# The end of an attention kernel rewritten: the last seven steps of the software pipeline in another order, a third buffer and other PSUM banks for the outputs

## The chip, the cores and the metric

The kernel runs on one core of one Trainium2 chip. The metric is the device time of one execution in microseconds (us). Before the change the median of three runs is 1626.83 us. An engine of the core (TensorE or PE, VectorE or DVE, ScalarE or ACT, GpSimd or POOL, SyncE or SP) works off its own instructions in the order in which they were emitted, and waits at an instruction until what that instruction needs is there.

## The reference

```python
x = L0_attn_x                                       # (2, 2048, 256), float32
x = x + rnn(layernorm(x), Wi, bi, Wh, bh)            # h = tanh(xt + h @ Wh.T + bh), along 2048 steps
x = x + ffn(layernorm(x), Wq, Wk, Ws, Wd, Wv, Wo)

# ffn: 8 heads of 64, 5 experts of which 2 are chosen
q, k = heads of x @ Wq, x @ Wk
wv = topk_mask(x @ Ws, 2) * sigmoid(x @ Ws)          # per token, head, expert
v = einsum('bthe,btek->bhtk', wv, einsum('btd,edk->btek', x, Wv))
probs = softmax(q * 64**-0.5 @ k.T)
attn = probs @ v
out = einsum('bthe,bthk,ekd->btd', topk_mask(x @ Wd, 2), attn, Wo)
```

## The kernel before

The first 130 us or so compute the recurrent part. Everything after it is attention, and it is one long software pipeline written out by hand: the order of the instructions in the program is the order in which each engine works.

**Units and steps.** There are 2 batches x 8 heads = 16 heads, and each head has 4 blocks of 512 queries: 64 units `u`. A unit works through the 2048 keys in 8 tiles `t` of 256 keys each (two halves of 128, side by side in a 128 x 1024 tile). A step `T` takes two such tiles, so a unit has `U_T` = 4 steps and there are `NT` = 256 steps with new scores, T = 0 to 255. A tile's way is:

- step T: `scores` (PE, line 634, into the PSUM pool `ps_s` of two buffers, tag "s"), `stage` (ACT copies the scores to SBUF, line 645), `largest` (DVE keeps a running maximum);
- after the unit's last tile: `turn_max`, `reduce_max`, `spread_max` turn the maxima into a 128 x 512 tile `top`. For the last unit the PSUM tile `pt` of it takes a buffer of "s", because no scores follow;
- step T+5: `subtract` takes the maximum off (line 693). POOL does most of them. DVE does the first two of each unit, and in the last unit every even one, reading `pt`;
- `exponential` (ACT, line 696): of the first tile of a pair at the end of step T+5, of the second at the start of step T+6;
- step T+6 (`LAG` = 6): `products` (PE, line 706: v times the probabilities, into `o`), and `fold` (POOL issues a DMA that adds one tile of a pair into the other, line 718), after which `sums` (PE, line 727) counts the denominators into `d` at every second step. The last unit has no folds; its sums go straight from the tiles.

So after the last scores at T = 255 there are seven more steps, T = 256 to 262, that only work off what is under way. In them the tiles 500 to 511 go through `products`; tiles 504 to 511 belong to the last unit, 63.

**Closing a unit.** `take` copies `o` to SBUF (lines 742, 743), `take_sums` the denominators (ACT line 749, DVE line 750). `close` calls `weigh`, which transposes the result (PE, line 759, tile `po` in a bank of the PSUM pool `misc`, two buffers) and forms the weights (DVE, lines 761 to 768), and multiplies them into `pro`, one copy for each expert (DVE, line 772). `gather` adds `pro` into `yd` in DRAM by a DMA, or, for the last head, adds it (POOL, line 817) to the tile `y` that `fetch_y` brought back (SP, line 793, 640 KB). For unit 63 `close_last` does it in four slices, each a product and an addition on DVE (lines 772 and 804).

**Outputs.** With the last head of a batch closed, each of its 16 chunks `c` of 128 tokens goes through `turn_out` and `project_out`. `turn_out(b, c)` makes three PE transposes of `y` into `py` (line 829, a `misc` bank), two ACT copies to SBUF (lines 833, 836), and issues on SP the load of the residual `z` (line 838, 128 KB). `project_out(b, c)` makes 24 matmuls into `pz` (line 846, a `misc` bank), the addition `z` = `pz` + `z` (DVE, line 854) and the store of `z` (SP, line 855, 128 KB). The tile `z` has two buffers: a load waits on SP until the store of the chunk two before it has landed, and SP's later transfers wait behind it.

**Order.** The lists `before`, `first_behind` and `behind` hold, for each step T, what is done before its products and behind its sums. For the last four units (chunks 0 to 15 of the second batch) the order before the change is:

| step T | before its products | behind its sums |
| --- | --- | --- |
| 256 | project 1 | `spread_max(63)`, close unit 61 |
| 257 | turn 2 | project 2, turn 3, gather unit 61 |
| 258 | project 3 | turn 4, fetch y of unit 62 |
| 259 | project 4 | take sums of unit 62, turn 5 |
| 260 | project 5 | close unit 62 |
| 261 | turn 6 | project 6, turn 7, gather unit 62, fetch y of unit 63 |
| 262 | project 7 | turn 8, turn 9, project 8, take sums and close unit 63, then turn and project the rest in turns, to chunk 15 |

`choose`, early in each batch, makes the experts' ranks: DVE writes the comparisons `later1` to `later4` (line 236), POOL counts them (lines 241, 242).

Of the kernel before, what the change touches and what calls it, by code (L numbers as in the profile page):

```python
# [8 lines left out]
F32 = mybir.dt.float32  # L9
# [5 lines left out]
P = 128  # L15
# [5 lines left out]
def rnn_then_switchhead_kernel(  # L21
# [15 lines left out]
    nc = tc.nc  # L37
    B, T, D = x.shape
    E, _, DH = Wv.shape
    H = Wq.shape[1] // DH  # L40
    KC = D // P
    NCH = T // P
    NP = H // 2
    QB = 512
    NQ = T // QB
    QS = QB // P
# [13 lines left out]
    for c in range(NCH):  # L60
        t = rconst.tile([P, B, D], F32, tag=f"x{c}", name=f"x{c}")
# [39 lines left out]
    o_chunks = [(i, min(P, ED - i)) for i in range(0, ED, P)]  # L101
# [18 lines left out]
    def misc(shape, nm):  # L120
        return ps_m.tile(shape, F32, tag="m", name=nm)
# [95 lines left out]
    def choose(pool, b, c0, n, half, nm, logits):  # L217

        gl = gates_all[:, c0 : c0 + n, b, half * HE : (half + 1) * HE]
        g = gl.rearrange("p c (h e) -> p c h e", e=E)
        nc.scalar.copy(logits, gl)
        g0 = logits.rearrange("p c (h e) -> p c h e", e=E)
        rank = pool.tile([P, n, H, E], F32, tag="rank", bufs=1, name=f"rank{nm}")
        nc.gpsimd.tensor_copy(
            rank.rearrange("p c h e -> p (c h) e"),
            ramp.unsqueeze(1).to_broadcast([P, n * H, E]),
        )
        if not half:  # L230
            sg = pool.tile([P, n, HE], F32, tag="sg", bufs=2, name=f"sg{nm}")
            nc.scalar.activation(sg, gl, AF.Tanh, scale=0.5)
        later = []
        for d in range(1, E):
            a = pool.tile([P, n, H, E - d], F32, tag=f"later{d}", bufs=1 + (d > 1), name=f"lt{nm}_{d}")
            nc.vector.tensor_tensor(a, g0[:, :, :, d:E], g[:, :, :, 0 : E - d], ALU.is_gt)
            later.append(a)

        def count(d):
            lo, hi = rank[:, :, :, 0 : E - d], rank[:, :, :, d:E]  # L240
            nc.gpsimd.tensor_tensor(lo, lo, later[d - 1], ALU.add)
            nc.gpsimd.tensor_tensor(hi, hi, later[d - 1], ALU.subtract)

        def take():
            rank_ = rank.rearrange("p c h e -> p c (h e)")
            if half:
                nc.gpsimd.tensor_scalar(gl, rank_, 1.5, None, ALU.is_lt)
                return

            nc.gpsimd.tensor_scalar(sg, sg, 0.5, 0.5, ALU.mult, ALU.add)  # L250
            nc.gpsimd.tensor_scalar(rank_, rank_, 1.5, None, ALU.is_lt)
            nc.gpsimd.tensor_tensor(gl, rank_, sg, ALU.mult)

        return [lambda d=d: count(d) for d in range(1, E)] + [take]
# [15 lines left out]
    with tc.tile_pool(name="prep", bufs=3) as pp, tc.tile_pool(  # L270
        name="lna", bufs=3
    ) as lnp, tc.tile_pool(name="ps_xi", bufs=3, space=PSUM) as ps_xi, tc.tile_pool(
        name="ps_t", bufs=3, space=PSUM
# [284 lines left out]
    LAG = U_T + 2  # L558
# [7 lines left out]
    NT = len(units) * U_T  # L566
# [121 lines left out]
    def subtract(t):  # L688
        u, c = t // HC, t % HC
        p = ring[t]  # L690
        last = u == len(units) - 1 and c % 2 == 0
        eng, top = (nc.vector, top_of[u][0]) if c < 2 or last else (nc.gpsimd, top_of[u][1])
        eng.tensor_tensor(p, p, top.unsqueeze(1).to_broadcast([P, 2, QB]), ALU.subtract)  # L693

    def exponential(t):
        nc.scalar.activation(ring[t], ring[t], AF.Exp)  # L696
# [95 lines left out]
        y_of[b, n] = four.tile([P, QS, E, DH], F32, tag="y", bufs=2, name=f"y{b}_{n}")  # L792
        nc.sync.dma_start(out=y_of[b, n], in_=yd[b, n])

    def close_last(u):

        i, n = units[u]
        b, _ = heads[i]
        po, mr = weigh(u)
        y = y_of[b, n]  # L800
        pr = four.tile([P, QS, E, DH], F32, tag="pro", bufs=1, name=f"pro{u}")
        for s in range(QS):
            masked(pr[:, s : s + 1], po, mr, s, 1)
            nc.vector.tensor_tensor(y[:, s], y[:, s], pr[:, s], ALU.add)

    def gather(u):

# [14 lines left out]
    for yT in yT_all:  # L822
        nc.gpsimd.memset(yT[:, len(o_chunks) - 1, :], 0.0)

    def turn_out(b, c):
        yf = y_of[b, c // QS][:, c % QS].rearrange("p e k -> p (e k)")
        py = misc([P, len(o_chunks), P], f"py{b}_{c}")
        for k, (r0, m) in enumerate(o_chunks):
            nc.tensor.transpose(py[0:m, k, :], yf[:, r0 : r0 + m], ident)
        yT = yT_all[yT_of["n"] % 2]  # L830
        yT_of["n"] += 1
        full = sum(m == P for _, m in o_chunks)
        nc.scalar.copy(yT[:, 0:full, :], py[:, 0:full, :])
        for k, (r0, m) in enumerate(o_chunks):
            if m < P:
                nc.scalar.copy(yT[0:m, k, :], py[0:m, k, :])
        z = ap.tile([P, D], F32, tag="z", name=f"z{b}_{c}")
        nc.sync.dma_start(out=z, in_=x1d[c, :, b, :])
        yT_of[b, c] = (yT, z)

# [75 lines left out]

    def at(table, T, f, *a):
        table.setdefault(T, []).append(lambda: f(*a))
# [58 lines left out]
    for u, (i, n) in enumerate(units):  # L977
        b, h = heads[i]
        T1 = (u + 1) * U_T
        at(first_behind, T1, spread_max, u)  # L980
        outs = [(b, n * QS + s) for s in range(QS)]
        if u == len(units) - 1:

            outs = [(b, c) for c in range(n * QS - QS, n * QS + QS)]
            todo = [(turn_out, *outs[0])]
            for k, o in enumerate(outs):
                todo += [(turn_out, *x) for x in outs[k + 1 : k + 2]] + [(project_out, *o)]
            at(behind, T1 + LAG - 1, fetch_y, u)
            for x in todo[:3] + [(take_sums, u), (close_last, u)] + todo[3:]:
                at(behind, T1 + LAG, *x)  # L990
            continue
        at(behind, T1 + LAG + 1, take_sums, u)
        at(behind, T1 + LAG + 2, close, u)
        at(behind, T1 + LAG + 3, gather, u)
        if h == H - 1:
            at(behind, T1 + LAG, fetch_y, u)
            if u < len(units) - 2:
                T = T1 + LAG + 4
                for o, t, p in zip(outs, (0, 1, 3, 3), (1, 2, 3, 4)):
                    at(before if o[1] % QS == 2 else behind, T + t, turn_out, *o)  # L1000
                    at(behind if o[1] % QS == 2 else before, T + p, project_out, *o)

    with tc.manual_schedule():
        for T in range(NT + LAG + 1):
            new = (2 * T, 2 * T + 1) if T < NT else ()
            sub = [t for t in (2 * (T - LAG + 1), 2 * (T - LAG + 1) + 1) if 0 <= t < 2 * NT]
            old = [t for t in (2 * (T - LAG), 2 * (T - LAG) + 1) if 0 <= t < 2 * NT]
            u_old = (T - LAG) // U_T - 1
            done = (T - LAG) % U_T == 0 and 0 <= u_old < len(units)
            fresh = sub and sub[0] % HC == 0  # L1010
            if done:
                take(u_old)
            if old:
                exponential(old[1])

            ss = [scores(t) for t in new]
            if new:
                stage(new[0], ss[0])
            if T % U_T == 0:
                if new:  # L1020
                    stage(new[1], ss[1])
                if 0 < T <= NT:
                    turn_max(T // U_T - 1)
                    reduce_max(T // U_T - 1)
                if new:
                    largest(new[1], ss[1])
            elif new:
                largest(new[1], ss[1])
                stage(new[1], ss[1])
            if fresh:  # L1030
                subtract(sub[0])
            if T % U_T and new:
                largest(new[0], ss[0])
            if fresh:
                subtract(sub[1])
            if sub and not fresh:
                subtract(sub[0])
            k = T - LAG
            if 0 < k < NT - U_T + 1:
                fold(2 * (k - 1))  # L1040
            if sub and not fresh:
                subtract(sub[1])
            for f in before.pop(T, []):
                f()
            for t in old:
                products(t)
            if 3 <= k and k % 2 and k - 3 < NT - U_T:
                t = 2 * (k - 3)
                sums(t, t + 2, t % HC == 0, t % HC != 0)
            if NT - 2 <= k < NT:  # L1050

                t0 = 2 * (NT - U_T)
                for t in range(t0, t0 + 4, 2) if k == NT - 2 else ():
                    sums(t, t + 1, t == t0, False)
                sums(2 * k, 2 * k + 1, False, k == NT - 1)
            if sub:
                exponential(sub[0])
            for f in first_behind.pop(T, []) + behind.pop(T, []):
                f()
        assert not before and not behind and not first_behind  # L1060
# [46 lines left out]
```

## Time and profile before

| what | value |
| --- | --- |
| three runs | 1624.53, 1626.83, 1630.81 us; median 1626.83 us |
| the profiled execution | 1623.28 us, its span in the profile 1621.5 us |
| mean granted TensorE clock | 0.992 of full speed |
| PE busy | 1539.0 us, 95% of the span |
| DVE, ACT, POOL busy | 1296.5, 1250.2, 1284.8 us (80%, 77%, 79%) |
| `z` loads | 32 of 128 KB, median 2.5 us from issue to landing |
| `z` stores | 32 of 128 KB, median 1.9 us |
| folds | 252 of 512 KB, median 6.2 us |
| `y` loads | 8 of 640 KB, median 6.8 us |

The profile is of one execution. A row of the timeline or of the groups gives the start, the duration, the engine, the line of the kernel, the operation, the tile written and the tile read, the shapes, and in square brackets how long the engine stood idle before it and who ended that. PEld is the loading of weights into PE, which overlaps its matmuls. A busy PE need not be a PE at its peak. "Landing" is the time from a DMA's issue to its completion.

### The profile page before, as it was taken

The numbers are of one execution on the slowest core, as the hardware profiler recorded it, in microseconds if no ns is written. First come the engines' busy times: TensorE is split into PE (matmuls) and PEld (weight loads), VectorE is DVE, ScalarE is ACT, GpSimd is POOL, SyncE is SP. The second block draws the span as 40 slices with busy tenths as digits, with TensorE's granted clock in tenths as the row PEclk, the third lists the DMA queues.
The fourth block names the chain that finished last, engine by engine and source line by source line (L and its number), as shares of the span: only waits on it lengthen the run. The fifth ranks groups of instructions, "written<-read, shape, count | busy, mean of one in ns | idle before, by whom it ended". The sixth has DMA issues, their size and how long they took to land.

```text
span 1621.5 us, 29233 instructions
## 1 busy us (share of the span) xinstructions
PE 1539.0 (95%) x11442; PEld 594.1 (37%) x11442; DVE 1296.5 (80%) x1807; ACT 1250.2 (77%) x1616; POOL 1284.8 (79%) x857
## 2 busy tenths in 40 slices
PE   6989899999999999998999999999999999999996
PEld 5974223333333333333333333333333333333333
DVE  7473789998988887777887768898888888988763
ACT  4664678888888888777887768888888888888862
POOL 3054688888888988888998768898889899998980
PEclk9999999999999999999999999999999999999999
DMA  5021368788888888677886767788888888889762
GB/s 161 1 106 37 106 141 193 176 188 173 178 172 172 173 168 172 139 166 143 180 182 156 174 148 178 168 169 174 169 172 169 178 160 177 168 174 186 153 134 86
DMA packets 86624, 252.27 MB, mean 156 GB/s; under 512 B 11920, under 2 KB 31184, under 8 KB 86480
## 3 DMA queue, kind: packets, MB, share of 16 engines
q0 software_dynamic: 43200, 163.60, 53.9%
q1 hardware_dynamic: 41648, 86.13, 17.6%
q8 instruction: 92, 1.51, 0.4%
q10 hardware_dynamic: 1632, 0.61, 0.1%
q14 instruction: 52, 0.43, 0.1%
HBM read 59.46 MB, written 50.33 MB: 68 GB/s over the span
## 4 chain that ended last, share of the span: by engine, by line
PE 64%; DVE 15%; DMA 6%; ACT 3%; issue 3%; POOL 1%; SPq 0%; DVEq 0%; ACTq 0%
PE s L634 23%; PE o L706 20%; DVE m L655 6%; PE d L727 6%; PE pq L159 4%; PE pk L140 3%; ACT p L645 3%; DMA xq<-xvd 2%; DMA p<-p 2%; PE pz L846 2%; DVE pro L772 2%; PE pt L683 2%; PE pm L668 1%; DVE p L693 1%; PE po L759 1%
## 5 line engine op out<-in xcount | busy, mean ns | idle before, releaser
L693 POOL TENSOR_TENSOR p<-p,top 128x1024 f32<-128x1024 f32 x381 | 1053.6, 3002 | 4.8 <-ACT top L686 4.6
L645 ACT COPY p<-s 128x1024 f32<-128x1024 f32 x512 | 511.0, 1011 | 161.4 <-DVE m L655 70.1
L696 ACT ACTIVATE p<-p 128x1024 f32<-128x1024 f32 x512 | 538.1, 1062 | 47.8 <-DVE p L693 38.1
L634 PE MATMUL s<-qs,k 64*128 64x512 f32 x1024 | 511.3, 617 | 7.7 <-ACT p L645 7.7
L634 PE MATMUL s<-q,k 64*128 64x512 f32 x1024 | 511.3, 617 | 6.7 <-ACT p L645 5.9
L706 PE MATMUL o<-p,v 128*32 128x512 f32 x4096 | 492.0, 597 | 8.5 <-DVE os L743 6.4
L655 DVE TENSOR_TENSOR m<-s,m 128x1024 f32<-128x1024 f32 x320 | 390.7, 1221 | 78.3 <-PE s L634 69.1
L718 POOL DMA_DIRECT2D p<-p x252 | 339.8, 1348 | 69.7 <-ACT p L696 22.9
L706 PEld LDWEIGHTS o<-p,v 128*32 128x32 f32 x4096 | 114.6, 109 | 297.2 <-issue 157.7
L634 PEld LDWEIGHTS s<-qs,k 64*128 64x128 f32 x1024 | 168.8, 185 | 145.3 <-issue 49.2
L634 PEld LDWEIGHTS s<-q,k 64*128 64x128 f32 x1024 | 168.8, 185 | 141.9 <-issue 49.6
L693 DVE TENSOR_TENSOR p<-p,pt 128x1024 f32<-128x1024 f32 x131 | 158.4, 1210 | 0.1
L727 PE MATMUL d<-p,ones 128*32 128x512 f32 x1040 | 151.5, 594 | 1.7 <-DMA p<-p 1.7
L655 DVE TENSOR_TENSOR m<-s,p 128x1024 f32<-128x1024 f32 x64 | 78.4, 1224 | 53.8 <-ACT p L645 53.4
L814 POOL DMA_DIRECT2D yd<-pro x48 | 43.3, 903 | 94.1 <-DVE pro L772 90.2
L619 DVE TENSOR_TENSOR xq<-xq,wp 128x1280 f32<-128x1280 f32 x60 | 89.2, 1487 | 28.3 <-DMA xq<-xvd 26.5
L772 DVE TENSOR_TENSOR pro<-po,mr 128x1280 f32<-128x1280 f32 (+1 forms) x67 | 95.9, 1431 | 2.7
L625 DVE TENSOR_REDUCE v<-xq 128x256 f32<-128x1280 f32 x60 | 88.6, 1476 | 0.0
L159 PE MATMUL pq<-xn2T,wq 128*32 128x512 f32 x512 | 66.8, 635 | 12.8 <-DVE xq L619 8.7
L727 PEld LDWEIGHTS d<-p,ones 128*32 128x32 f32 x1040 | 37.8, 110 | 91.9 <-issue 77.0
L140 PE MATMUL pk<-xn2T,wk 128*32 128x512 f32 x512 | 61.5, 598 | 0.7 <-ACT q L169 0.7
L673 DVE TENSOR_REDUCE mq<-pm 128x4 f32<-128x512 f32 x64 | 44.3, 692 | 19.2 <-PE pm L668 17.8
(175 smaller groups left out, 1472.4 us busy)
## 6 DMA issues: line engine op xcount, KB each, us to landing
p<-p POOLq DMA_DIRECT2D x252, 512.0 KB, 6.2
xq<-xvd SPq DMA_DIRECT2D x60, 640.0 KB, 5.2
yd<-pro POOLq DMA_DIRECT2D x48, 640.0 KB, 7.5
qs<-q SPq DMA_DIRECT2D x64, 128.0 KB, 2.7
yd<-pro SPq DMA_DIRECT2D x8, 640.0 KB, 4.1
y<-yd SPq DMA_DIRECT2D x8, 640.0 KB, 6.8
x<-in_x SPq DMA_DIRECT2D x16, 256.0 KB, 5.5
x1d<-x SPq DMA_DIRECT2D x16, 256.0 KB, 2.0
```

Of the source, the lines that this page charges most:

```text
L140: nc.tensor.matmul(pk[at_col : at_col + 32], lhsT=wk[:, kc, h * DH + g : h * DH + g + 32], rhs=xc[:, kc, c0 // 2 : (c0 + HC) // 2, o, :], ...
L159: nc.tensor.matmul(pq[at_col : at_col + 32, :], lhsT=wq[:, kc, h * DH + g : h * DH + g + 32], rhs=xn2T[:, kc, b, n * QB : (n + 1) * QB], s ...
L619: nc.vector.tensor_tensor(xq, xq, wp.unsqueeze(2).to_broadcast([P, 4, DH, E]), ALU.mult)
L634: nc.tensor.matmul(ss[:, o, :], lhsT=k_of[i][half, c, :], rhs=q_of[i, n][o][half, :], start=True, stop=True,)
L645: nc.scalar.copy(p, ss)
L655: nc.vector.tensor_tensor(m, ss, ring[t - 1] if c == 1 else m, ALU.max)
L693: eng.tensor_tensor(p, p, top.unsqueeze(1).to_broadcast([P, 2, QB]), ALU.subtract)
L696: nc.scalar.activation(ring[t], ring[t], AF.Exp)
L706: nc.tensor.matmul(o_of[u][at_col : at_col + 32, :], lhsT=v_of[i][:, 2 * c + o, g : g + 32], rhs=ring[t][:, o, :], start=c == 0, stop=c == ...
L718: nc.gpsimd.dma_start(out=ring[t], in_=ring.pop(t + 1), accum_op=ALU.add)
L727: nc.tensor.matmul(den_of[u][32 * g : 32 * (g + 1), :], lhsT=ones32, rhs=ring[(t, t1)[g // 2]][:, g % 2, :], start=first, stop=last, tile_ ...
L772: nc.vector.tensor_tensor(dst, po[:, s : s + n, 0:DH].unsqueeze(2).to_broadcast([P, n, E, DH]), mr[:, s : s + n].unsqueeze(3).to_broadcast ...
```

## The change

Only the order of the last seven steps and the buffers they use are changed; what is computed is the same.

- The exponentials of both tiles of a step follow their subtractions in the same step (T = 257, 258). At T = 259 the subtractions of tiles 508 to 511 are all made, and their four exponentials; T = 260 has none.
- Unit 61 is gathered at T = 256 and not 257; unit 62 is closed and gathered at T = 259, in the step of its sums, and not at 260 and 261. The `y` of unit 63 is fetched at T = 260 and not 261.
- Outputs go in pairs: chunks 4 and 5 are turned behind T = 258 and projected at 259, 6 and 7 at 259 and 260, 8 and 9 at 260 and 261, 10 and 11 at 261 and 262. Chunks 12 to 15 follow the closing of unit 63.
- The transposes `py` of chunks 4, 6, 8, 10 and 12 to 15 go to the two "s" buffers of the scores' pool; chunks 5, 7, 9 and 11 stay in `misc`.
- `z` has three buffers and not two; `later4` has one and not two.

```diff
--- before.py
+++ after.py
@@ -232,7 +232,7 @@
             nc.scalar.activation(sg, gl, AF.Tanh, scale=0.5)
         later = []
         for d in range(1, E):
-            a = pool.tile([P, n, H, E - d], F32, tag=f"later{d}", bufs=1 + (d > 1), name=f"lt{nm}_{d}")
+            a = pool.tile([P, n, H, E - d], F32, tag=f"later{d}", bufs=1 + (1 < d < 4), name=f"lt{nm}_{d}")
             nc.vector.tensor_tensor(a, g0[:, :, :, d:E], g[:, :, :, 0 : E - d], ALU.is_gt)
             later.append(a)
 
@@ -792,7 +792,7 @@
         y_of[b, n] = four.tile([P, QS, E, DH], F32, tag="y", bufs=2, name=f"y{b}_{n}")
         nc.sync.dma_start(out=y_of[b, n], in_=yd[b, n])
 
-    def close_last(u):
+    def close_last(u, outs):
 
         i, n = units[u]
         b, _ = heads[i]
@@ -802,6 +802,11 @@
         for s in range(QS):
             masked(pr[:, s : s + 1], po, mr, s, 1)
             nc.vector.tensor_tensor(y[:, s], y[:, s], pr[:, s], ALU.add)
+        for s in range(QS):
+            turn_out(*outs[s], True)
+            if s:
+                project_out(*outs[s - 1])
+        project_out(*outs[-1])
 
     def gather(u):
 
@@ -822,9 +827,14 @@
     for yT in yT_all:
         nc.gpsimd.memset(yT[:, len(o_chunks) - 1, :], 0.0)
 
-    def turn_out(b, c):
+    def turn_out(b, c, spare=False):
         yf = y_of[b, c // QS][:, c % QS].rearrange("p e k -> p (e k)")
-        py = misc([P, len(o_chunks), P], f"py{b}_{c}")
+        if spare:
+
+            py = ps_s.tile([P, 2, QB], F32, tag="s", name=f"py{b}_{c}")[:, 0, : len(o_chunks) * P]
+            py = py.rearrange("p (k n) -> p k n", n=P)
+        else:
+            py = misc([P, len(o_chunks), P], f"py{b}_{c}")
         for k, (r0, m) in enumerate(o_chunks):
             nc.tensor.transpose(py[0:m, k, :], yf[:, r0 : r0 + m], ident)
         yT = yT_all[yT_of["n"] % 2]
@@ -834,7 +844,7 @@
         for k, (r0, m) in enumerate(o_chunks):
             if m < P:
                 nc.scalar.copy(yT[0:m, k, :], py[0:m, k, :])
-        z = ap.tile([P, D], F32, tag="z", name=f"z{b}_{c}")
+        z = ap.tile([P, D], F32, tag="z", bufs=3, name=f"z{b}_{c}")
         nc.sync.dma_start(out=z, in_=x1d[c, :, b, :])
         yT_of[b, c] = (yT, z)
 
@@ -980,25 +990,34 @@
         at(first_behind, T1, spread_max, u)
         outs = [(b, n * QS + s) for s in range(QS)]
         if u == len(units) - 1:
-
-            outs = [(b, c) for c in range(n * QS - QS, n * QS + QS)]
-            todo = [(turn_out, *outs[0])]
-            for k, o in enumerate(outs):
-                todo += [(turn_out, *x) for x in outs[k + 1 : k + 2]] + [(project_out, *o)]
-            at(behind, T1 + LAG - 1, fetch_y, u)
-            for x in todo[:3] + [(take_sums, u), (close_last, u)] + todo[3:]:
-                at(behind, T1 + LAG, *x)
+            at(behind, T1 + LAG - 2, fetch_y, u)
+            at(behind, T1 + LAG, take_sums, u)
             continue
         at(behind, T1 + LAG + 1, take_sums, u)
+        if h == H - 1:
+            at(behind, T1 + LAG, fetch_y, u)
+        if u == len(units) - 2:
+            at(behind, T1 + LAG + 1, close, u)
+            at(behind, T1 + LAG + 1, gather, u)
+            continue
         at(behind, T1 + LAG + 2, close, u)
+        if u == len(units) - 3:
+            at(behind, T1 + LAG + 2, gather, u)
+            continue
         at(behind, T1 + LAG + 3, gather, u)
         if h == H - 1:
-            at(behind, T1 + LAG, fetch_y, u)
-            if u < len(units) - 2:
-                T = T1 + LAG + 4
-                for o, t, p in zip(outs, (0, 1, 3, 3), (1, 2, 3, 4)):
-                    at(before if o[1] % QS == 2 else behind, T + t, turn_out, *o)
-                    at(behind if o[1] % QS == 2 else before, T + p, project_out, *o)
+            T = T1 + LAG + 4
+            for o, t, p in zip(outs, (0, 1, 3, 3), (1, 2, 3, 4)):
+                at(before if o[1] % QS == 2 else behind, T + t, turn_out, *o)
+                at(behind if o[1] % QS == 2 else before, T + p, project_out, *o)
+
+    last = [(B - 1, c) for c in range(NCH - 3 * QS, NCH)]
+    for k in range(0, 2 * QS, 2):
+        T = NT + 2 + k // 2
+        for o in last[k : k + 2]:
+            at(behind, T, turn_out, *o, o[1] % 2 == 0)
+            at(behind if T == NT + LAG - 1 else before, T + 1, project_out, *o)
+    at(behind, NT + LAG, close_last, len(units) - 1, last[2 * QS :])
 
     with tc.manual_schedule():
         for T in range(NT + LAG + 1):
@@ -1010,7 +1029,7 @@
             fresh = sub and sub[0] % HC == 0
             if done:
                 take(u_old)
-            if old:
+            if old and T < NT + 2:
                 exponential(old[1])
 
             ss = [scores(t) for t in new]
@@ -1033,13 +1052,17 @@
                 largest(new[0], ss[0])
             if fresh:
                 subtract(sub[1])
-            if sub and not fresh:
+            if sub and not fresh and T < NT + LAG - 2:
                 subtract(sub[0])
             k = T - LAG
             if 0 < k < NT - U_T + 1:
                 fold(2 * (k - 1))
-            if sub and not fresh:
+            if sub and not fresh and T < NT + LAG - 2:
                 subtract(sub[1])
+            if T == NT + LAG - 3:
+
+                subtract(sub[0] + 2)
+                subtract(sub[1] + 2)
             for f in before.pop(T, []):
                 f()
             for t in old:
@@ -1053,8 +1076,13 @@
                 for t in range(t0, t0 + 4, 2) if k == NT - 2 else ():
                     sums(t, t + 1, t == t0, False)
                 sums(2 * k, 2 * k + 1, False, k == NT - 1)
-            if sub:
+            if sub and T < NT + LAG - 2:
                 exponential(sub[0])
+            if NT < T < NT + LAG - 2:
+                exponential(sub[1])
+            if T == NT + LAG - 3:
+                exponential(sub[0] + 2)
+                exponential(sub[1] + 2)
             for f in first_behind.pop(T, []) + behind.pop(T, []):
                 f()
         assert not before and not behind and not first_behind
```

## The prediction

> **What bounds the kernel now.** I read the page, the stretches around the end, the waits of the last stretch, the chain of waits, and the timeline of the last 65 us. The page first:
>
> ```profile
> span 1621.5 us, 29233 instructions
> PE 1539.0 (95%) x11442; PEld 594.1 (37%) x11442; DVE 1296.5 (80%) x1807; ACT 1250.2 (77%) x1616; POOL 1284.8 (79%) x857
> ```
>
> PE fills the span, so an edit of the end is worth what PE stands idle there. T = 256 begins near 1556.5 us; the last sums (T = 261) end at 1588.33 (issued 1587.29, 1.04 long). The two stretches:
>
> ```profile
> 1556.50:1588.33 31.83, 29.16 (x306) 11.96 (x306) 14.65 (x22) 16.48 (x27) 18.68 (x11) 1.00 0.55 130
> 1588.33:1621.50 33.17, 20.72 (x272) 10.23 (x263) 9.73 (x23) 5.86 (x20) 2.23 (x1) 0.90 0.29 96
> ```
>
> The columns are the length, then PE, PEld, DVE, ACT and POOL busy, clock, DMA share, GB/s. In the first stretch PE idles 2.7 us, in the second 12.5. What it waits for there, from the waits of the second stretch and the chain:
>
> ```profile
> DVE z L854 <- DMA z<-x1d: 13.1, 6, 3.1
> SPq L838 <- DMA out<-z: 11.3, 7, 1.9
> ```
>
> ```profile
> 1611.15 2.13 DMA out<-z
> ...
> 1613.35 0.32 SPq L838
> ...
> 1613.71 2.24 DMA out<-z
> ...
> 1615.96 2.05 DMA z<-x1d
> ...
> 1618.14 0.42 DVE z L854
> ```
>
> Two `z` buffers make a ring: store lands (2.1), load goes out (0.35) and lands (2.1), addition (0.45), store. That is 5.0 us for two chunks, 2.6 for one, where PE needs 0.49 for a turn and 1.43 for a projection (their pieces in the chain): 1.92. A third buffer, outputs moved into the steps, and a shorter closing all attack this stretch. The price stands in the first one, which is nearly full.
>
> **The sum, first to the end of the last sums.** *Work moved forward:* before, chunks up to 5 are projected and up to 6 turned by then; after, 9 and 9. That is 4 x 1.43 + 3 x 0.49 = 7.2 us of PE. Rows for the waits:
>
> ```profile
> 1566.21 0.14 PEld L727 LDWEIGHTS d<-p,ones 128*32 128x32 f32 x4 [1.21 <-DMA p<-p]
> 1569.56 1.50 PE L846 MATMUL pz<-wo,yT 128*32 128x256 f32 x24 [0.52 <-ACT yT L833]
> 1579.04 0.58 ACT L749 COPY os<-d 64x512 f32<-64x512 f32 x1
> 1579.65 0.68 DVE L750 TENSOR_TENSOR os<-d,os 64x512 f32<-64x512 f32 x1 [2.06 <-ACT os L749]
> 1586.03 1.49 DVE L772 TENSOR_TENSOR pro<-po,mr 128x1280 f32<-128x1280 f32 x1
> 1587.66 2.90 POOL L817 TENSOR_TENSOR y<-y,pro 128x1280 f32<-128x1280 f32 x1 [12.48 <-DVE pro L772]
> ```
>
> *Waits taken away.* Behind turns 3, 4 and 5 PE waits 0.52 us each for the ACT copy: 1.6 in all. The sums of T = 257 wait 1.2 for the fold issued at 1559.02, which took 7.2 us; the two before it, alone under way, took 5.1 and 4.9. Gather 61 now stands ahead of the next fold in POOL's queue, which moves that fold from 1561.97 to 1567.3 (1564.37 + 2.92), so the first should land by 1564.2. I take the whole 1.2; the other end is 0.
>
> *Waits added.* (1) Turn 3's copies stand behind the exponential of tile 505: wait 0.75. (2) ACT makes the exponentials of 506 and 507 (about 1 us each) before the copies of turns 4 and 5, and PE has nothing else: 0.8; pair 8, 9 finds ACT free: 0.1. (3) Closing unit 62 one step ahead: its transposes must wait for the sums through the ACT copy 0.58, DVE's 0.68 and three hand-overs of about 0.1: 1.55 us, with turns 6 and 7 and both projections queued behind on PE. Before, a whole step lay between. (4) Projection 6 takes the `misc` bank that `po` of unit 62 holds until DVE has made `pro`: 2.9 us from the transposes' start (1584.64 to 1587.52), of which PE fills 0.60 + 2 x 0.49: 1.35. Sum 4.55.
>
> DVE, where the additions of chunks 4 and 5 precede take_sums, and SP, where the 640 KB of `y` now precede both their loads, set the bounds of (3). Loads here took 2.2 to 6.1 us. The fetch goes out near 1572 (behind chunk 3's store of 1573.24, less the 1.2 above); with the 5.1 us that this `y` took and 0.6 behind it, 4 lands at 1577.7, additions 4 and 5 end by 1578.6, and DVE takes the sums at 1579.3: 0.7 to spare. A slow one adds up to 1.5. At the other end (3) and (4) could vanish if PE comes late anyway. So the last sums end at 1588.33 + 7.2 + 4.55 - 1.6 - 1.2 = 1597.3.
>
> **From there to the end.** Before: 33.2. After: turns 10, 11 (0.98), copy (0.1), projections 10, 11 (2.86), which hide take and take_sums (3.9 on ACT and DVE); then chunk 10's addition frees the bank and `po` starts at +4.1 with 0.60 + 0.1; weights 0.7 (1598.45 to 1599.15); first slice 0.46 + 0.46 (0.93 a slice, steps of L772); turn 12 at +6.5; turn 13 waits for slice two, ends +7.9. PE is then bound: 4 x 1.43 + 2 x 0.49 = 6.7, +14.6; addition 0.55, +15.1; the end 2.95 later, as from 1618.56 to 1621.5. Sum 18.1. With loads landing in 2.1 us, those of chunks 12 and 13 are there over 2 us before they are wanted, 14's 0.85 and 15's (which waits for 12's store) 0.35. The span becomes 1597.3 + 18.1 = 1615.4, 6.1 less. The own time of the profiled execution is 1623.28 (1.8 beside the span), 3.5 below the median; the same 6.1 off the median gives **1620.7 us**.
>
> **The parts at nothing.** Subtractions 509 to 511: POOL stood idle 12.48 us from 1575.17, the row above; with its slowest, 3.6 instead of 2.44, exponential 511 would hold take_sums by up to 2. Fold 502 right behind fold 500: at 7.2 they land by 1575.4, wanted near 1577.6 (1576.88 before, plus projection 5's 1.43, less 1.2, plus 0.5 of waits). Spare banks: with all `py` in `misc` I would count 0.8 more. `later4`: POOL was done with it at 150.53, DVE writes it again after 153.08; elsewhere there are 9 us or more.
>
> [...] Two stretches of about 4.5 us (closing 62, closing 63) hold nothing on PE but transposes and waits. The rows of before:
>
> ```profile
> 109.69:113.10 3.41, 2.18 (x16) 1.46 (x14) 3.28 (x6) 2.52 (x6) 2.96 (x4) 1.00 0.20 77
> 113.10:116.51 3.41, 2.20 (x18) 1.87 (x18) 2.30 (x5) 1.21 (x3) 0.00 (x0) 1.00 0.41 154
> 1594.49:1597.90 3.41, 1.07 (x19) 0.53 (x12) 1.11 (x2) 0.56 (x1) 0.00 (x0) 1.00 0.38 128
> 1597.90:1601.31 3.41, 2.74 (x22) 1.48 (x24) 2.62 (x8) 0.53 (x2) 0.00 (x0) 0.50 0.16 49
> ```
>
> With 1.07 of 3.41 us busy the clock halved for the next 3.41; with 2.18, transposes alone, it did not; a window with 1.52 (649.00 to 652.41) did not either. Idle time in one new window is at most 1.8 or 2.2 us, so 1.6 or 1.2 us busy: near the edge. I count nothing; a halved window costs at most 1.7 us. [...]
>
> **Rivals.** *A: the tail's DMA chain is dearer than this profile shows.* The runs scatter by 6.3 us and the median is 3.5 above the profiled one. Some 13 of the last 15 us of the chain are DMA latency, which after has slack. If the whole 3.5 sits there, the gain is 9.6: 1617.2. Against it: 1590 other microseconds can scatter too. *B, slower: loads 4 and 5 are late behind `y` of unit 62.* DVE stands at addition 4, and take_sums, closing 62 and all of PE stand behind it. `y` at the median 6.8 and then a load at 6.1 is 12.9 from 1572, so 1584.9, two additions to 1585.7: take_sums 6.4 us late, plus a halved clock window 1.7: 8.1 lost against 6.1 gained, 1628.8. It decides from a landing of chunk 4's `z` 11 us after the fetch. For it: two folds are in flight; against: 5.1 was measured for this `y`. *C: the new waits eat the gain.* No gain at the fold (1.2), POOL slow (2), one halved window (1.7): 1.2 gained, 1625.6. The diff leaves none of its parts undone, that I see.
>
> **How the numbers follow.** My forecast has 0.53, A 0.30, C 0.09, B 0.08. A measurement of this kernel can tell about 0.5%, 8.1 us, from no change, so the forecast itself (6.1) and C lie within it. A falls below 1618.7; a forecast with waits (3) and (4) gone, 9.0, would too, and gets 0.03 of its 0.53. Faster by over 0.5%: 0.33. Slower by over 0.5% (above 1635.0) needs B at more than its price, late at the next pair too: 0.05 of its 0.08. The rest is 0.62. The range goes from 1615.5 (A, and half of (3) and (4) gone) to 1627.0 (C and some of B).
>
> **What would show it.** Right: no wait of SP for `out<-z` and at most 1 us of DVE waiting for `z` after the last sums; PE's end near +14.6 from them; PE waiting about 1.5 us at `po` of unit 62 and 1.4 at projection 6; the fold of 1559 landing in about 5 us. Wrong: last sums later than 1599 (B, C), a clock of 0.5 anywhere between 1576 and 1612, turn 12 waiting for the fourth slice and not the first (2.8 us more), or a gain that the traces' last 65 us do not hold.

## The result, and the profile after

The changed kernel takes 1624.38 us (median of 22 runs) where the kernel before, in 22 runs of its own, takes 1626.68: ratio 0.9985, 95% interval 0.9973 to 0.9997. That is 2.3 us of the 6.1 that were predicted: inside the range and inside the 0.5%, on the forecast side, with about four tenths of the forecast size. The interval, 0.5 to 4.4 us of gain, leaves out the 6.1.

The profiled execution of after has a span of 1622.6 us, 1.1 more than that of before. This is no contradiction: the time ahead of the last steps varies by more than the tail. In the fourteen profiles of this document the last unit's maxima are turned (`turn_max`, T = 256) anywhere from 1557.0 to 1564.1 us, while the tail from there to the end repeated to about 0.2 us in the two profiles that each of the two kernels has (before 64.49 and 64.63, after 63.31 and 63.10). So everything below is measured as **tail**: from the first of those transposes to the end of the span. By it the change brings 1.4 us (means of the two) where the prediction's sum said 6.1 (58.4).

The two stretches of after, cut at the end of the last sums as for before; columns: length, then PE, PEld, DVE, ACT, POOL busy, clock, DMA share, GB/s:

```profile
1559.32:1603.03 43.71, 36.18 (x403) 16.51 (x402) 16.32 (x26) 17.75 (x33) 20.40 (x11) 0.96 0.53 131
1603.03:1622.60 19.57, 13.48 (x167) 6.75 (x166) 8.07 (x19) 4.18 (x14) 0.00 (x0) 0.91 0.23 76
```

The second stretch shrank from 33.2 to 19.6, nearly as worked out (18.1). The first grew by 12.4, from 31.3 to 43.7, and 9.0 was worked out. Its waits on PE, and SP's wait on stores over the whole tail:

```profile
PE po L759 <- DVE os L750: 2.6, 1, 2.6
PE pz L856 <- DVE z L864: 2.5, 1, 2.5
```

```profile
SPq L848 <- DMA out<-z: 0.6, 2, 0.4
```

The ring of two buffers is gone (11.3 us of SP waiting before, 0.6 after). Two waits of PE for DVE, 2.5 and 2.6 us, are new. The chain of waits of after shows what stands behind both (in parts; dots stand for what lies between):

```profile
1561.30 7.04 DMA p<-p
...
1575.83 1.94 issue
1577.77 0.44 DVE z L864
...
1579.67 5.35 DMA z<-x1d
...
1585.15 0.42 DVE z L864
...
1585.60 0.69 DVE os L750
...
1586.34 0.84 PE po L759 x4
```

The fold of 1561.30 takes 7.0 us as before, so the predicted gain at this fold is missing. Then the chain goes twice through the addition of a `z` (line 864), both times late. The timeline at the first of them (rows picked out):

```profile
1569.52 1.76 POOL L718 DMA_DIRECT2D p<-p  x2
1571.66 1.25 SPq L848 DMA_DIRECT2D z<-x1d  x1
1577.77 0.42 DVE L864 TENSOR_TENSOR z<-pz,z 128x256 f32<-128x256 f32 x1 [3.48 <-issue]
1578.34 2.80 PE L856 MATMUL pz<-wo,yT 128*32 128x256 f32 x48 [2.52 <-DVE z L864]
```

Two folds are issued as a pair (x2), 2.1 and 1.6 us before the load of chunk 3's `z`. The first lands in 4.6 us, the second in 7.2, at 1577.3; the load lands 0.4 us behind that, 6.0 us after its issue. The same load took 3.2 before. DVE stands at its addition (idle 3.48), PE stands 2.52 us at projection 4, whose bank it frees, and SP can send chunk 3's store, the 640 KB of `y` and the loads of chunks 4 and 5 only after it. These two land 5.6 and 5.4 us after their issue, just behind the `y`, and DVE comes late to unit 62's sums.

The clock halved twice, at unit 62's and at unit 63's closing. The windows ahead of and in each:

```profile
1583.27:1586.68 3.41, 0.78 (x9) 0.34 (x4) 1.49 (x3) 0.58 (x1) 0.00 (x0) 1.00 0.19 66
1586.68:1590.10 3.42, 2.75 (x21) 1.80 (x23) 2.02 (x4) 1.05 (x4) 0.55 (x1) 0.50 0.37 105
1607.17:1610.58 3.41, 1.21 (x9) 0.71 (x9) 2.80 (x9) 0.47 (x2) 0.00 (x0) 1.00 0.49 156
1610.58:1613.99 3.41, 3.41 (x28) 1.28 (x28) 1.57 (x5) 0.64 (x3) 0.00 (x0) 0.50 0.01 3
```

PE was busy 0.78 and 1.21 us of 3.41, and the next 3.41 us ran at 0.50. In the second, projection 12 takes 2.79 us and not 1.50.

### The profile page after: what moved, and what is told of

It reads as the page before. It is cut to its first block, busy times and chain, and to the rows that moved or that the text cites. A ratio compares the mean times of both kernels' runs of the same rounds, so it can differ in the third digit from the quotient of the medians.

```text
span 1622.6 us, 29228 instructions
## 1 busy us (share of the span) xinstructions
PE 1542.2 (95%) x11442; PEld 597.1 (37%) x11442; DVE 1297.2 (80%) x1807; ACT 1250.1 (77%) x1616; POOL 1284.5 (79%) x857
## 4 chain that ended last, share of the span: by engine, by line
PE 66%; DVE 14%; DMA 6%; ACT 3%; issue 3%; POOL 1%; SPq 0%; DVEq 0%; ACTq 0%
PE s L634 23%; PE o L706 20%; PE d L727 6%; DVE m L655 5%; PE pq L159 3%; PE pk L140 3%; DMA xq<-xvd 3%; ACT p L645 2%; PE pz L856 2%; DMA p<-p 2%; PE pt L683 2%; PE pm L668 2%; PE po L759 1%; DVE pro L772 1%; DVE p L693 1%
```

## The experiments

Two theories went into them. **Theory 1:** the early gather of unit 61 pairs two folds, the pair delays the small `z` loads, and the in-order queues of DVE, SP and PE pass that on. **Theory 2:** closing unit 62 in the step of its sums costs PE the time, whatever the transfers do.

**Both kernels once more.**

> The kernel before, unchanged, for one more profile. The measure of this study is the tail: from the first transpose of the last unit's maxima (T = 256) to the end of the span, 64.5 us in the profile of before and 63.3 in that of after. Both theories expect 64.5 within about 0.7 here; a wider miss means that single tails can't be compared at 1 us.

> The changed kernel, unchanged, for one more profile. If the order of the queues sets the tail it is 63.3 within about 0.7 again, with PE waiting about 2.5 us at projection 4 for the addition of chunk 3 and 2.6 at the transposes of unit 62. If those two waits were chance of one execution, they shrink towards 0.8 and 1.5 and the tail towards the predicted 58.4.

Before: tail 64.63. After: tail 63.10, with the same waits of 2.55 and 2.47 us. So the waits are not chance of one execution, and by these two pairs single tails can be compared to some tenths, except where the granted clock is halved in one and not in the other. Every run below has one profile, so its tail stands on one execution.

**The gather put back by a step.**

```diff
-            at(behind, T1 + LAG + 2, gather, u)
+            at(behind, T1 + LAG + 3, gather, u)
```

> The changed kernel with unit 61 gathered at T = 257 again, so that POOL issues the next fold ahead of it, about 5 us earlier, and not right before the next fold. Theory 1 (the two folds issued together at 1569.5 and 1570.4 keep the small load of chunk 3's z on the way for 6.0 us; DVE stands at its addition, PE behind it): that load lands in about 3.2 us as before, the wait of PE at projection 4 falls from 2.5 to about 0.8, the y load and chunks 4 and 5 go out about 3 us earlier, and the tail is 60 to 61.5. Theory 2 (closing unit 62 in the step of its sums is what costs, whatever the transfers do): the tail stays within 0.7 of 63.3, and what is not waited for at projection 4 is waited for at unit 62's transposes.

Tail 59.63; 1619.85 us, ratio 0.9965 (0.9950 to 0.9980). The timeline:

```profile
1566.82 1.74 POOL L718 DMA_DIRECT2D p<-p  x1
1572.13 0.86 POOL L718 DMA_DIRECT2D p<-p  x1
1574.09 1.21 SPq L848 DMA_DIRECT2D z<-x1d  x1
1579.06 2.80 PE L856 MATMUL pz<-wo,yT 128*32 128x256 f32 x48 [0.81 <-ACT yT L843]
1586.34 0.66 PE L759 MATMUL po<-ident,os 128*128 128x128 f32 x4 [1.91 <-DVE os L750]
```

The folds go out 5.3 us apart, chunk 3's load lands in 3.5 us, projection 4 waits 0.81 us for its copy and no longer for DVE, unit 62 1.91. One line of the schedule is worth about 3.5 us of the tail: 2.4 of waits on PE, and the halved clock at unit 62, which is not there now: its four transposes take 0.66 us, and 0.84 in after. Theory 1 holds; of theory 2 the wait of about 1.5 us remains that the prediction has as its wait (3). The last sums end at +39.97 after the first transpose; the prediction's 1597.3 is +40.3.

**The same line alone, on the kernel before.**

```diff
-        at(behind, T1 + LAG + 3, gather, u)
+        at(behind, T1 + LAG + 3 - (u == len(units) - 3), gather, u)
```

> The kernel before with nothing but unit 61 gathered at T = 256, the step that the prediction counted as a gain of 1.2 us at the fold of 1559. Theory 1 says the fold gains nothing (it took 7.0 us in the changed kernel too), the next two folds go out together, chunk 3's z lands in about 6 instead of 3.2 us, and PE waits about 2 us longer for its addition: last sums at +33 instead of +31, tail 66 to 67. The prediction's own reading: last sums at +30, tail 63.3.

```profile
1571.88 1.78 POOL L718 DMA_DIRECT2D p<-p  x2
1580.73 2.79 PE L846 MATMUL pz<-wo,yT 128*32 128x256 f32 x24 [3.03 <-DVE z L854]
```

Tail 68.02, 3.5 more than before; last sums at +34.85; chunk 3's load landed in 6.2 us, PE stood 3.03 us and not 0.52, and the 24 matmuls behind that took 2.79 us and not 1.50, as projection 12 did at the clock of 0.50 in after. So the step costs 3.5 us on either kernel (here in one execution), and the fold ahead of it took 6.9 us and gained nothing.

**The `z` loads two chunks ahead.**

```diff
+        tag = "xl" if b == B - 1 and c % 5 > 2 else "z"
+        z_of[b, c] = ap.tile([P, D], F32, tag=tag, bufs=2 if tag == "xl" else 3, ...)
+        nc.sync.dma_start(out=z_of[b, c], in_=x1d[c, :, b, :])
...
+        for k in (c,) if b < B - 1 else (0, 1, 2) if c == 0 else (c + 2,) if c + 2 < NCH else ():
+            load_z(b, k)
```

> The changed kernel with the z loads of the second batch issued two chunks earlier each, into five buffers (three and two others that are free by then). Theory 1: no addition waits for its z, PE's wait at projection 4 falls to about 0.8 and at the transposes of unit 62 to about 1.55, the tail is 59.5 to 61. Theory 2: the wait at unit 62's transposes stays above 2.3, tail 61.5 to 63. If the clock halves at unit 62 and 63 all the same, about 1.3 us of the loss stays in either case.

Tail 57.40; 1620.85 us, ratio 0.9967 (0.9951 to 0.9983). The gather still stands early here and the folds still go out as a pair; one of the loads even takes 7.0 us. But nobody waits for it: PE stands 0.81 us at projection 4 and 1.42 at unit 62, whose transposes take 0.66 us, and 0.84 in after, where the clock halved in them. So the fold pair does no harm by itself. It costs time where a small load goes out behind it only one step before DVE needs that load.

**The third `z` buffer alone (with `later4` in one buffer), on the kernel before.**

```diff
-            a = pool.tile([P, n, H, E - d], F32, tag=f"later{d}", bufs=1 + (d > 1), name=f"lt{nm}_{d}")
+            a = pool.tile([P, n, H, E - d], F32, tag=f"later{d}", bufs=1 + (1 < d < 4), name=f"lt{nm}_{d}")
...
-        z = ap.tile([P, D], F32, tag="z", name=f"z{b}_{c}")
+        z = ap.tile([P, D], F32, tag="z", bufs=3, name=f"z{b}_{c}")
```

> The kernel before with nothing but the third z buffer (and later4 with one). By the prediction's reading the two-buffer ring sets the last 25 us of before, so this alone must take most of what the whole change was to take there: tail 60 to 61 against 64.5, no wait of SP for a store above 0.5, last sums still at +31. Rival: PE, ACT and the misc banks give the same 2.6 us a chunk without the ring; then the tail stays above 63.5.

Tail 61.18: 3.4 us less than before, and 2 us better than the whole change. Last sums at +31.62. SP's wait for stores falls to the closing 0.9 us at the program's end. The reading of the ring was right, its price a little under what I expected. So the rest of the change, taken together, costs the tail about 2 us.

**Unit 62 closed one step ahead alone, on the kernel before.**

```diff
-        at(behind, T1 + LAG + 2, close, u)
-        at(behind, T1 + LAG + 3, gather, u)
+        ahead = u == len(units) - 2
+        at(behind, T1 + LAG + 2 - ahead, close, u)
+        at(behind, T1 + LAG + 3 - ahead, gather, u)
```

> The kernel before with nothing but unit 62 closed and gathered one step ahead, in the step of its sums. Theory 2 and the prediction's added wait (3): PE stands about 1.5 us longer, for DVE's sum, at unit 62's transposes; the last sums move from +31.1 to +32.6 and the tail from 64.5 to about 66. If the wait is free because PE is waiting for other things there, the tail stays at 64.5.

```profile
1587.36 0.66 PE L759 MATMUL po<-ident,os 128*128 128x128 f32 x4 [2.00 <-DVE os L750]
```

PE stands 2.00 us at the transposes and no longer 0.52 at projection 5, a net 1.48; last sums at +32.80, 1.5 to 1.9 later. The tail is 68.58, 4.0 more. The other 2.1 to 2.6 us lie behind the last sums (35.8 and not 33.2 to 33.7): in this execution the last loads and stores of the two-buffer ring were slow (chunk 14's addition waited 3.0 us for its load, chunk 15's load went out 4.1 us after the store it waits for). One execution can't say whether that is more than scatter.

**PE kept busy at unit 63's closing.**

```diff
+        idle = ps_o.tile([P, QB], F32, tag="d", name="idle")
+        for _ in range(2):
+            nc.tensor.matmul(idle, lhsT=ident, rhs=wq[:, 0, :], start=True, stop=True)
```

> The changed kernel with two full matmuls of no use (128x128 by 128x512, into the free bank d) between unit 63's transposes and turn 12, where PE stood idle 1.8 us and the clock was halved for the 3.4 us after. If idle time sets the clock, it is not halved behind unit 63, projection 12 takes 1.5 and not 2.8 us, and the tail falls from 63.2 to about 62; if the halving comes from transposes counting for nothing, the matmuls help just the same, so this prices the halving, and the counting is read from the windows. If the halving costs nothing because DVE's slices are last, the tail stays at 63.2.

```profile
1608.92:1612.33 3.41, 3.14 (x22) 1.35 (x15) 2.79 (x9) 0.00 (x0) 0.00 (x0) 1.00 0.33 98
1612.33:1615.74 3.41, 3.03 (x41) 1.52 (x43) 2.87 (x7) 1.20 (x5) 0.00 (x0) 1.00 0.19 61
```

The clock stays at 1.00 there, projection 12 takes 1.50 us, and from the last sums to the end it is 18.36 us, with the two added matmuls in it, and not 19.5: the halving costs 1.2 us or a little more. The tail falls by only 0.4, to 62.83, because in this execution the last sums end at +44.47 and not +43.65. Its mean granted clock is 0.989, that of after 0.992; how much of the 0.8 us is the clock's was not shown.

**All transposed outputs back in the `misc` banks.**

```diff
-        if spare:
+        if spare and False:
```

> The kernel with the early z loads, but every transposed output in the misc banks again. The prediction counted 0.8 us for the spare banks: tail 57.4 + 0.8 = 58.2, more (to 60) since chunks 12 to 15 lose theirs too. If the two misc banks do, 57.4 within 0.4.

Tail 62.38 against 57.40 for the kernel it is made from, one profile of each: by these the spare banks are worth 5.0 us, above the range expected. The last sums come 1.1 later (+40.57 against +39.51), the rest takes 21.80 and not 17.89. The mean granted clock of the two profiled executions is 0.991 and 0.993, and how much of the 5.0 is the clock's, the runs don't say.

**Two exponentials back in the following step.**

```diff
-            if old and T < NT + 2:
+            if old and T < NT + LAG - 3 + 1:
...
-            if NT < T < NT + LAG - 2:
+            if T == NT + LAG - 3:
                 exponential(sub[1])
```

> The kernel with the early z loads, but the exponentials of tiles 505 and 507 at the start of the following step again, behind the copies of the turns. The prediction's waits (1) and (2) say that the exponentials ahead of the copies cost PE up to 0.25 at projection 3 and 0.8 at projection 4: the wait at projection 4 shrinks to 0.5 or less and the tail by 0.3 to 0.8. If instead the earlier exponentials are what lets ACT be free for unit 62's sums, PE waits longer at unit 62's transposes and the tail is 57.4 to 58.5.

```profile
1578.30 2.80 PE L863 MATMUL pz<-wo,yT 128*32 128x256 f32 x48 [0.19 <-ACT yT L850]
1585.09 0.66 PE L759 MATMUL po<-ident,os 128*128 128x128 f32 x4 [1.42 <-DVE os L750]
```

Projection 4 waits 0.19 and not 0.81 us, unit 62 as long as without the edit, and the tail is 57.10, 0.3 less. Having the exponentials in the step of their subtractions brings nothing in these two steps. Whether it costs the 0.3 us, one profile of each kernel can't say.

**A version from the two causes.** The early loads go into `z` and two buffers of the same size that were last read near 625 us. Here they are joined with the gather put back, turns 6 and 7 ahead of unit 62's transposes, projections 6 and 7 behind the products of T = 260, projections 10 and 11 beside the closing of 63, whose transposes take the free bank "o" (part of the diff):

```diff
         for s in range(QS):
             masked(pr[:, s : s + 1], po, mr, s, 1)
             nc.vector.tensor_tensor(y[:, s], y[:, s], pr[:, s], ALU.add)
+            if s in (1, 2):
+                project_out(*beside[s - 1])
```

> A version built from the two causes: z loads two chunks ahead, unit 61's gather back at T = 257, turns 6 and 7 ahead of unit 62's sums and closing, projections 6 and 7 behind the products of T = 260, take_sums of 63 ahead of the copies of chunks 10 and 11, whose projections run beside unit 63's weights and slices, its transposes in the free bank o. Theory 1: 57.4 as with the early z loads, less about 1.0 at unit 62's transposes, 0.8 at projection 6 and 2 at the closing of 63: a tail of 53.5 to 55, ratio near 0.994. If the waits only change places, 56 to 57.5.

Tail 57.42, ratio 0.9947 (0.9930 to 0.9964): no better a tail than with the early loads alone. PE stood 2.1 us at unit 62's transposes, since I had put ACT's copies of turns 6 and 7 ahead of its copy of the sums; the 16 matmuls of the products behind it took 3.13 us, and 1.90 in the steps before and after. The waits had changed places, as the second expectation has it.

> The best version with one order mended: in it ACT made the copies of turns 6 and 7 ahead of unit 62's sums, and PE stood 2.1 us there. Now the sums are taken first, then turns 6 and 7, then the closing. If PE's stand at the transposes of 62 is the path ACT copy, DVE sum, hand-overs (1.55 us) less the two turns (0.98), it falls to about 0.6, and without a halved clock the tail is 53.5 to 55; with one halved window behind it 1.7 more. Rival: the time has gone to the order of DVE, then the stand stays above 1.5 and the tail at 57.

```profile
1581.30 0.65 PE L762 MATMUL po<-ident,os 128*128 128x128 f32 x4 [0.62 <-DVE os L750]
```

```profile
1557.19:1595.33 38.14, 35.01 (x403) 15.46 (x402) 16.44 (x27) 18.15 (x34) 20.39 (x11) 1.00 0.59 151
1595.33:1611.50 16.17, 11.62 (x167) 6.41 (x166) 7.75 (x19) 3.56 (x13) 0.00 (x0) 1.00 0.23 76
```

With that one order mended: tail 54.31, 10.2 us less than before; 1616.44 us, ratio 0.9938 (0.9917 to 0.9959). PE is busy 46.6 of the 54.3 us at the full clock. It has the shortest tail and the lowest median of the kernels here, and by the intervals it is faster than before and than the change; its interval overlaps those of the three other versions with early loads or the gather put back.

## Why the prediction was right, and where it was wrong

Direction and class were right: a small gain, not to be told from no change by 0.5%. Its size was not: the range reached from 11 us of gain to no gain at all, so lying in it says little, and the interval leaves out the 6.1. The step that failed is named in the sum: *"Gather 61 now stands ahead of the next fold in POOL's queue ... I take the whole 1.2"*.

- **That term has the wrong sign.** I took the two short folds (5.1 and 4.9 us) for the rule and the 7.2 for the effect of the fold behind it. With that fold moved away it still took 7.0 and 6.9 us. Nor were 1.2 us to be had there: the row that the prediction reads is that of PEld. PE itself had sums of other tiles to do and stood 0.30 us, as the sum of its waits in that stretch (2.7) would have shown. What the step did was to pair the next two folds ahead of a small load: +3.5 us, shown by its removal from after and by its addition to before. I had asked of the moved fold only whether its own reader would wait, not what else was on the DMA engines when it went out. PE's own row of before at the fold:

```profile
1566.21 0.62 PE L727 MATMUL d<-p,ones 128*32 128x512 f32 x2 [0.30 <-DMA p<-p]
```

- **The rest of the first sum holds roughly.** Without that step the last sums end at +39.97; the sum without the 1.2 gives 41.5, so its other terms are 1.5 too high together. In after: 31.31 + 7.2 of work moved + 4.47 more of waits (6.97 against 2.50, PE's gaps over 0.3 us) + 0.7 = 43.7. The 0.7 left over is not the whole price of the halved window: the kernel with the gather put back has 2.35 less of such waits, no halved clock there (0.66 us for the four transposes of unit 62 and not 0.84), and ends its last sums 3.75 sooner. So the window took about 1.4 (estimate), and the work moved was less than 7.2 by about 0.7. Wait (3), 1.55, measured 1.48 alone and 1.42 with early loads; wait (2), 0.8, measured 0.81; wait (1), 0.75, was 0.52; wait (4), 1.35, was 0.67 to 0.78, and not for the bank that it names: in after projection 6 began at 1589.13, while DVE read `po` of unit 62 until 1589.41, and the profile has turn 7's second copy as what ended the wait. (The 6.1 us that the prediction gives for the slowest load is a store; the slowest `z` load there took 5.9.)
- **From the last sums on** 18.1 measured 19.5 in after, with a halved clock, and 17.9 in two of the kernels with early loads. Turn 12 waited for the first slice, as taken. The halving was counted at nothing with 1.7 as its bound; it cost 1.2 here. "Near the edge" was a fair reading of the rows at hand and nothing the wrong value. The prediction worked out 1.2 and 1.6 us busy for its two stretches of transposes. In after, 1.21 us of transposes alone, at unit 63, were followed by 3.41 us at 0.50, and so were 0.78 us of sums and transposes at unit 62. More of transposes alone, 2.18 us in before and 1.89 in after, was followed by 1.00. Near 167 us of after 1.62 us, 1.28 of them transposes, were followed by 0.50, while 1.52 us of other matmuls (the prediction's window of 649.00) were followed by 1.00; whether that is because they were transposes was not shown. The two stretches of after, near 112 and near 167 us:

```profile
112.12:115.53 3.41, 1.89 (x12) 1.18 (x12) 3.31 (x5) 1.91 (x4) 2.09 (x2) 1.00 0.37 138
115.53:118.94 3.41, 2.68 (x22) 2.41 (x22) 1.20 (x4) 0.79 (x3) 0.00 (x0) 1.00 0.20 77
166.74:170.15 3.41, 1.62 (x10) 0.83 (x8) 2.86 (x3) 2.41 (x4) 0.00 (x0) 1.00 0.00 0
170.15:173.56 3.41, 2.05 (x16) 0.90 (x20) 1.07 (x4) 0.04 (x1) 2.62 (x3) 0.50 0.00 0
```

- **The spare banks** were priced at 0.8 for chunks 4 to 11 and measured 5.0 for all of them, the clock's part in it not shown. I had left out chunks 12 to 15; 3.9 of the 5.0 lie behind the last sums, where those are worked off.
- **Rivals.** C came out (1.4 gained in the tail; it said 1.2 and had 0.09): nothing at the fold and halved windows, though the third part was the late `z` and not a slow POOL. B's mechanism was there at about a sixth of the 6.4 us that it gave: chunk 4's load landed with the `y` and unit 62 waited 1.1 us longer. A fell: the median gained less than the sum, not more.

## What to carry to other kernels

Moving a transfer's issue is not done with when its own reader still gets it in time: list what else is issued in the next few microseconds, and which in-order engine stands at the slowest of those. A small load that an in-order engine needs belongs several steps ahead, into a buffer that is free by then; here that took 5.8 us off the tail of after, where the whole change had taken 1.4. And when a wait is filled by work of another engine (turns on PE), check whose copies that work puts ahead of the thing waited for.

## What the runs showed of the hardware

- In the profiles of before and after, a 128 KB load of `z` in the tail took 2.0 to 2.4 us with no fold and no `y` load on its way (16 loads). Issued 1.6 to 1.7 us behind a fold that itself took 7.0 to 7.2 us, it took 5.8 to 6.0 us and landed 0.4 us behind that fold (three loads). Of the two folds that after issued 0.6 us apart the first landed in 4.6 us, the second in 7.2.
- In after the granted clock was 0.50 for 3.41 us behind each of the two stretches of 3.41 us in which PE was busy 0.78 and 1.21 us. Projection 12 took 2.79 us there, and 1.50 at a clock of 1.00 in the run with PE kept busy ahead of it.
